# ScalarE's first guess of reciprocal roots at two seams of a fused two-layer kernel, moved transposes, and sums moved from GpSimd to VectorE

## The chip, the cores and the metric

The kernel runs on one core of a Trainium2 chip. The metric is the device time of one execution, in microseconds (us). The kernel before took 3251.36 us, the median of three executions (3250.76 to 3253.78).

The engines of the core are named as the profile names them: PE (TensorE, matrix products and transposes; PEld is its weight load), DVE (VectorE), ACT (ScalarE), POOL (GpSimd) and SP (SyncE, which here only issues DMAs).

## The reference

Two layers follow each other on x, 32 sequences of 128 tokens with 512 channels each, all float32.

```python
# layer 0
h   = ln(x) + silu(cond) @ W_ada.T            # one shift per sequence
q, k, v = h @ Wqkv.T                          # 16 heads of 64; q and k are normalised per head
x   = x + softmax(q k / 8) v @ Wout.T
tok = x.reshape(4096, 512)
gate = softmax(tok @ Wgate.T)                 # 8 experts
vals, idx = top_k(gate.T, 512)                # each expert takes its best 512 tokens
g   = ln(tok[idx])
y   = gelu_tanh(g @ fc1[e].T) @ fc2[e].T      # 512 -> 2048 -> 512, for each expert e
tok = tok.at[idx].add(y * vals)
# layer 1
n   = ln(x) * (1 + scale1) + shift1           # scale, shift = cond @ w_adaln1.T, per sequence
x   = x + attention(n) @ wo.T                 # 16 heads of 32
n   = ln(x) * (1 + scale2) + shift2
x   = x + gelu(n @ w1.T) @ w2.T               # 512 -> 2048 -> 512
```

Every `ln` needs the reciprocal square root of (variance + 1e-5) of each token; the change concerns how some of these are computed.

## The kernel before

**Stages.** Layer 0's attention goes by pairs of sequences. Then the router finds each expert's 512 tokens. Then come the experts 0 to 7 (function `expert(e, after)`), and then layer 1 in 16 groups of two sequences each (function `group(g)`). The stage of the experts begins at about 1086 us of the span, layer 1 at about 1916 us. At both seams the products of the next stage need the results of the last DMAs of the one before, so that PE has nothing else to do.

**Order of the work.** The kernel is written as a list of operations: each has its engine or engines (with an estimate of its time), what it reads and writes, and a priority. A planner (class `Sched`) goes through this list when the program is built, and gives each engine a fixed order of instructions. Where an operation may go to one of two engines (`also`), the planner chooses by its estimates. So an edit of one operation's priority or engine can move others too. The helper `tt` (L1106) makes an elementwise sum or difference of two tiles on DVE or on POOL; all of them appear in the profile with the line L1109 (DVE) or L1110 (POOL). All transposes have the line L1085.

**Normalisation.** `normed` (L311) takes a list of tiles of 128 tokens. For each it does the statistics (L317, L318, on DVE), then for all tiles of the list together variance + eps (L320) and `newton` (L293): a first guess of the reciprocal root by integer arithmetic on the bits of the float (L299), and three rounds of Newton's method of three operations each (L303, L305, L307). These are ten small operations on DVE in a chain, on one column per tile. The tile is then normalised (L1796 in the experts, xng; L2127 in layer 1, a_0n and so on), transposed by PE in four blocks of 128x128 (tpg; a_0t), and the four blocks are copied from PSUM with scale and shift by DVE and ACT in turn (L1806 and L1808, gT; L2137 and L2139, nT and n2T).

**An expert.** Four tiles xg of 128 tokens each are gathered by indirect DMAs that POOL issues (L1740). Expert 0's tiles are normalised in two pairs (names ng_0 and ng_1 in the profile), those of the later experts in one list of four. The two matrix products are done with seven block products in place of eight. So there are sums of blocks beside them: of gT (tg, the four sums at L1814 to L1817), of the fc1 weights (s, four POOL sums for each quarter m, L1763 to L1766), of the fc2 weights (t, L1785 to L1788: twelve sums t1, t2 and fc2_12 per expert, all on POOL), and of the products' results (h and hs). The first matrix goes in four quarters m = 0 to 3; a quarter is seven products u1, u2, u6, u7, u5, u4, u3 (L1838, PE, eight matmuls each), which DVE combines in the same order (v and h, L1843). ACT does the gelu (L1849), and the h and hs sums follow. The second matrix is the down products d (L1902), 32 matmuls each. Within expert 0 DVE also makes the token lists of the later experts (`expert_tokens`, L1666: oh L1684, pi on PE L1704, idx L1710), and the norms and transposes of expert 1.

**The seam into layer 1.** The scale and shift of all sequences come from products of the condition (pad), which are copied to pads, transposed by PE (ptd), and evicted with bias by four DVE operations (ss, L2029). `bias0` (L2109) is eight matmuls pb for the output bias, which DVE adds to bo_t (L2112). `norm_T` (L2122) is the normalisation, transposition and eviction of a group's two sequences; it stands before the attention (a1, dst nT) and before the MLP (a2, dst n2T, whose first product is m, L2363).

## Time and profile before

The profiled execution took 3251.28 us, of which 3249.5 us are the span that the profile shows.

| what | value |
|---|---|
| median of three executions | 3251.36 us |
| profiled execution, its span | 3251.28 us, 3249.5 us |
| mean clock granted to PE | 0.995 |
| PE busy | 98% of the span, 21786 matmuls |
| DVE, ACT, POOL busy | 69%, 29%, 22% |
| largest waits of PE | 11.9, 11.9, 5.3, 4.2, 1.4 us |
| span time of the first product of expert 0, of the first qk of layer 1 | 1101.02 us, 1923.56 us |

The busy row of the page gives for each engine its busy time and its share of the span. The table of waits names for an engine, its operation and line, what it waited for: the total, how often and the longest. The timeline gives the start of a piece of work from the span's start, its duration, and in brackets how long the engine had been idle before it and what ended that. A window gives the busy time of each engine in a stretch of the span, then the clock that PE was granted (1.00 is full speed), the share of DMA time and the GB/s moved. Numbers of buffers are left out of the names: ng_0 in the profile stands for the first norms of expert 0 and ng_1 for its second pair and for those of expert 1.

### The profile page before, as it was taken

Reading aid. Unit: us, or ns where it says so; the run is one execution under the profiler, and the core shown is the slowest. Engines: PE = TensorE matmul, PEld = TensorE weight load, DVE = VectorE, ACT = ScalarE, POOL = GpSimd, SP = SyncE. Lnnn points to the kernel's source line nnn. Section 1 sums busy time; section 2 is a strip of 40 time slices with the busy share of each in tenths; the row PEclk is TensorE's granted clock in tenths of the full one; section 3 lists DMA queues with packets and bytes.
Section 4 is the critical chain, followed back from the end, with each engine's and each line's share of the span. In section 5 each row is a group of like instructions: output and inputs, shape, how many; then the busy total and the mean of one; then the engine's idle time right before and its main releaser. Section 6 shows DMA issues by size and latency. Waiting matters only on the chain. (4 is left out here: it accounts for less than half of the span.)

```text
span 3249.5 us, 55816 instructions
## 1 busy us (share of the span) xinstructions
PE 3198.8 (98%) x21786; PEld 2556.4 (79%) x21786; DVE 2251.1 (69%) x4849; ACT 956.6 (29%) x2292; POOL 713.4 (22%) x563
## 2 busy tenths in 40 slices
PE   8999999999999899999999999999999999999999
PEld 4665666555557788888888878999999999999998
DVE  7877776978677888656666547666666666666665
ACT  3333333344431122221222213333333333333332
POOL 0111111000024457766676510000000000000000
PEclk9999999999999899999999999999999999999999
DMA  4122112221125523434333462333333333333343
GB/s 172 53 80 65 62 56 80 87 85 63 61 78 195 169 76 100 120 107 120 92 107 104 138 203 90 106 101 102 101 103 102 101 98 99 101 102 102 104 137 105
DMA packets 247122, 335.39 MB, mean 103 GB/s; under 512 B 22082, under 2 KB 156738, under 8 KB 246338
## 3 DMA queue, kind: packets, MB, share of 16 engines
q1 hardware_dynamic: 239394, 314.30, 29.7%
q0 software_dynamic: 7168, 16.91, 2.8%
q8 instruction: 174, 2.85, 0.4%
q14 instruction: 98, 0.80, 0.1%
q10 hardware_dynamic: 288, 0.52, 0.1%
HBM read 277.01 MB, written 54.66 MB: 102 GB/s over the span
## 5 line engine op out<-in xcount | busy, mean ns | idle before, releaser
L2318 POOL TENSOR_TENSOR hi_t<-hi_t,inv 128x512 f32<-128x512 f32 x32 | 40.7, 1273 | 1225.9 <-DVE inv L1120 1225.9
L2374 ACT ACTIVATE m<-m,prm 128x128 f32<-128x128 f32 x512 | 162.0, 390 | 235.8 <-DVE m L2368 235.7
L1902 PE MATMUL d<-fc,h 128*128 128x256 f32 x992 | 219.0, 380 | 0.6 <-DVE v L1843 0.6
L1902 PEld LDWEIGHTS d<-fc,h 128*128 128x128 f32 x992 | 187.9, 190 | 26.1 <-DVE v L1843 0.8
L1849 ACT ACTIVATE h<-h,prm 128x256 f32<-128x256 f32 x256 | 114.9, 500 | 259.8 <-DVE h L1843 259.7
L1838 PE MATMUL u<-gT,fc 128*128 128x256 f32 x768 | 178.6, 383 | 1.0 <-ACT gT L1808 1.0
L1838 PEld LDWEIGHTS u<-gT,fc 128*128 128x128 f32 x768 | 147.3, 192 | 21.8 <-ACT gT L1808 1.4
L2368 DVE TENSOR_TENSOR m<-mu,m 128x512 f32<-128x512 f32 x128 | 87.9, 687 | 106.8 <-PE m L2363 104.0
L1284 ACT ACTIVATE sq<-qk 128x512 f32<-128x512 f32 x128 | 80.7, 632 | 232.1 <-DVE qk L1322 227.9
L2368 DVE TENSOR_TENSOR mu<-mu,m 128x512 f32<-128x512 f32 x96 | 65.9, 686 | 88.2 <-PE m L2363 88.2
L2363 PE MATMUL m<-n2a,w_s 128*128 128x128 f32 x1024 | 124.9, 275 | 0.0
L2424 PE MATMUL n<-w_t,m 128*128 128x256 f32 x512 | 123.0, 379 | 0.0
L1838 PE MATMUL u<-tg,s 128*128 128x256 f32 x512 | 120.9, 379 | 0.9 <-DVE tg L1109 0.9
L2363 PE MATMUL m<-n2T,w 128*128 128x128 f32 x1024 | 119.8, 275 | 1.4 <-ACT n2T L2139 1.4
L1843 DVE TENSOR_TENSOR h<-v,u 128x512 f32<-128x512 f32 x128 | 86.3, 681 | 48.8 <-PE u L1838 47.3
L2363 PEld LDWEIGHTS m<-n2T,w 128*128 128x128 f32 x1024 | 118.2, 192 | 2.4 <-ACT n2T L2139 1.6
L2363 PEld LDWEIGHTS m<-n2a,w_s 128*128 128x128 f32 x1024 | 119.5, 192 | 0.0
L2424 PE MATMUL n<-w_t,ms 128*128 128x256 f32 x512 | 117.8, 382 | 0.0
L1318 PE MATMUL q<-wqkv,hT 128*128 128x512 f32 x240 | 114.6, 608 | 0.4 <-DVE oT L1470 0.4
L2424 PE MATMUL n<-w,m 128*128 128x256 f32 x512 | 114.7, 382 | 0.0
L1318 PE MATMUL q<-wqkv,hsb 128*128 128x512 f32 x240 | 113.9, 597 | 0.1
L1902 PE MATMUL d<-t,hs 128*128 128x256 f32 x512 | 113.4, 379 | 0.0
(1161 smaller groups left out, 7501.2 us busy)
## 6 DMA issues: line engine op xcount, KB each, us to landing
w_t<-t2d SPq DMA_DIRECT2D x256, 256.0 KB, 3.3
w<-in_w_dram SPq DMA_DIRECT2D x192, 256.0 KB, 4.8
fc<-in_fc_dram SPq DMA_DIRECT2D x64, 512.0 KB, 4.7
fc<-in_fc_dram SPq DMA_DIRECT2D x32, 1024.0 KB, 5.5
x<-in_x_dram SPq DMA_DIRECT2D x32, 256.0 KB, 3.4
xT<-in_xT_dram SPq DMA_DIRECT2D x32, 256.0 KB, 2.7
otd<-oT SPq DMA_DIRECT2D x32, 256.0 KB, 2.1
ol<-otd SPq DMA_DIRECT2D x32, 256.0 KB, 3.5
```

The costliest lines, as they stand in the source:

```text
L1284: sch.op(ACT, act_us(D), lambda: nc.scalar.activation(sq.t, qk[i][j].t, AF.Square), w=[sq], r=[qk[i][j]], prio=pr, job=job)
L1318: nc.tensor.matmul(ps[m].t, lhs()[:, k, :], rhs[0](k), start=(k == 0), stop=(k == 1))
L1838: nc.tensor.matmul(ps[n].t[:, t, :], lhs()[:, k, t * P : (t + 1) * P], rhs.t[:, k, :], start=(k == 0), stop=(k == 1))
L1843: sch.op(DVE, dve_us(D), lambda: nc.vector.tensor_tensor(o_.t, a_.t, ps[n].t, ALU.add), w=[o_], r=[a_, ps[n]], prio=pr, job=job)
L1849: sch.op(ACT, act_us(HQ, 1), lambda t=t, c=c: nc.scalar.activation(o_.t[:, t, :], o_.t[:, t, :], AF.Gelu_apprx_tanh, bias=col("b1s", e * 1 ...
L1902: nc.tensor.matmul(ps[n].t[:, j, :], lhs[m].t[:, k, t * P : (t + 1) * P], rhs.t[:, 2 * m + k, :], start=(m == 0 and k == 0), stop=(m == NM ...
L2318: sch.op(POOL, pool_us(D), lambda inv=inv: nc.gpsimd.tensor_tensor(hi_b.t, hi_b.t, flat(inv), ALU.add), w=[hi_b], r=[inv], prio=pr + 197, ...
L2363: nc.tensor.matmul(ps[n].t[:, u, :], l1w[what].t[:, k, (NQ * q + u) * P : (NQ * q + u + 1) * P], rhs()[:, k, :], start=(k == 0), stop=(k = ...
L2368: sch.op(DVE, dve_us(D), lambda: nc.vector.tensor_tensor(o_.t, a_.t, ps[n].t, ALU.add), w=[o_, *more], r=[a_, ps[n]], prio=pq_, job=job)
L2374: sch.op(ACT, act_us(S, 1), lambda u=u, c=c: nc.scalar.activation(o_.t[:, u, :], o_.t[:, u, :], AF.Gelu, bias=col("b1", c), scale=1.0), w= ...
L2424: nc.tensor.matmul(ps[n].t, Ah[lhs][c // NQ].t[:, c % NQ, :], b_.t[:, k, :], start=(c == 0), stop=(c == 7))
```

## The change

1. A new function `guessed` computes the first guess with two operations of ACT, Ln of the variance and Exp of -0.5 times that (both scaled by a power of two), and one round of Newton on DVE. It takes the place of the integer guess and three rounds, in expert 0's norms, and in both norms of group 0 of layer 1. There the tiles are also handled one by one and no longer in pairs, but for expert 0's tiles 2 and 3. The variances are gathered in `seen` and added to a flag tile (hi_b) that is read at the kernel's end.
2. In expert 0, the transposes of tiles 2 and 3 get an earlier place on PE (directly behind u1 and u2 of m = 0), the gsel copies a later one (behind the tg sums), and the tg sums stay on DVE.
3. The twelve t sums of expert 0 go from POOL to DVE, at a priority of the first products. The planner in turn gives seven h and hs sums of m = 0 and 1 to POOL.
4. The statistics of expert 1's tiles wait for expert 0's last tg sum, and its transposes get a later priority: they come behind the first down products of expert 0.
5. At the seam into layer 1, `bias0` is split in two halves with the transposes ptd between them, the ss evictions come behind the norms of group 0, and the bo_t addition comes later. An empty ACT operation makes the table of Exp be loaded behind the copies to pads.

```diff
@@ -310,3 +310,22 @@
-    def normed(self, srcs, name, pr, job, cols=D):
+    def guessed(self, mv, v, n, name, pr, job):
+        nc, sch = self.nc, self.sch
+        z, y, t = self.sml(name + "z", n), self.sml(name + "y", n), self.sml(name + "t", n)
+        us = dve_us(n)
+        var = lambda: mv.t.rearrange("p (n two) -> p n two", two=2)[:, :, 1]
+        sch.op(ACT, 0.3, lambda: nc.scalar.activation(z.t, var(), AF.Ln, bias=self.lnc[:, 0:1], scale=2.0**-32),
+               w=[z], r=[mv], prio=pr, job=job, table="exp")
+        sch.op(ACT, 0.3, lambda: nc.scalar.activation(y.t, z.t, AF.Exp, bias=self.lnc[:, 1:2], scale=-0.5),
+               w=[y], r=[z], prio=pr, job=job, table="exp")
+        sch.op(DVE, us, lambda: nc.vector.scalar_tensor_tensor(t.t, y.t, -0.5, y.t, ALU.mult, ALU.mult),
+               w=[t], r=[y], prio=pr, job=job)
+        sch.op(DVE, us, lambda: nc.vector.tensor_tensor(t.t, t.t, v.t, ALU.mult),
+               w=[t], r=[t, v], prio=pr, job=job)
+        sch.op(DVE, us, lambda: nc.vector.scalar_tensor_tensor(y.t, t.t, 1.5, y.t, ALU.add, ALU.mult),
+               w=[y], r=[t, y], prio=pr, job=job)
+        return y
+    def normed(self, srcs, name, pr, job, cols=D, act=False, after=()):
@@ -316,3 +335,3 @@
             st = self.sml(f"{name}st{i}", 6)
-            sch.op(DVE, dve_us(D), lambda st=st, s=s: nc.vector.bn_stats(st.t, s.t[:, :cols]), w=[st], r=[s], prio=pr, job=job)
+            sch.op(DVE, dve_us(D), lambda st=st, s=s: nc.vector.bn_stats(st.t, s.t[:, :cols]), w=[st], r=[s, *after], prio=pr, job=job)
             sch.op(DVE, 0.17, lambda st=st, i=i: nc.vector.bn_aggr(mv.t[:, 2 * i : 2 * i + 2], st.t),
@@ -322,2 +341,5 @@
             w=[v], r=[mv], prio=pr, job=job)
+        if act:
+            self.v = v
+            return mv, self.guessed(mv, v, n, name, pr, job)
         return mv, self.newton(v, n, name, pr, job)
@@ -1035,2 +1057,8 @@
     nc.vector.memset(ones_f, 1.0)
+    st.lnc = const_tile("lnc", (P, 2))
+    nc.vector.memset(st.lnc[:, 0:1], EPS * 2.0**-32)
+    nc.vector.memset(st.lnc[:, 1:2], -16 * math.log(2.0))
+    seen = const_tile("seen", (P, 8))
+    nc.vector.memset(seen, 0.0)
+    seen_b = stands(seen)
     iota_j = const_tile("iota_j", (P, P), I32)
@@ -1724,2 +1752,10 @@
+    seen_v = []
+    def saw(pr, job, after):
+        for v, at, n in seen_v:
+            sch.op(DVE, 0.15, lambda v=v, at=at, n=n: nc.vector.tensor_scalar(seen[:, at : at + n], v.t, 2.0**-32, None, ALU.mult),
+                   w=[(seen_b, at)], r=[v, *after], prio=pr, job=job)
+        seen_v.clear()
     def expert(e, after):
@@ -1768,3 +1804,3 @@
         if e:
-            mv, y = st.normed(xg, f"ng_{e}", pe_, job, cols=D)
+            mv, y = st.normed(xg, f"ng_{e}", pe_, job, cols=D, after=sums0 if e == 1 else ())
             stat = [(mv, y, h) for h in range(NH)]
@@ -1772,5 +1808,8 @@
             stat = []
-            for z in range(2):
-                mv, y = st.normed(xg[2 * z : 2 * z + 2], f"ng_{e}_{z}", pe_ + z, job, cols=D)
-                stat += [(mv, y, h) for h in range(2)]
+            def norm0(hs, pr, after=()):
+                mv, y = st.normed([xg[h] for h in hs], f"ng_{e}_{hs[0]}", pr, job, cols=D, act=True, after=after)
+                stat.extend((mv, y, i) for i in range(len(hs)))
+                seen_v.append((st.v, hs[0], len(hs)))
+            norm0((0,), pe_ - 3)
+            norm0((1,), pe_ - 3)
         if 0 < e < E - 1:
@@ -1788,7 +1827,12 @@
                 tt(lambda o_=o_, hs=hs: o_.t[:, hs, :], lambda a_=a_, hs=hs: a_.t[:, hs, :], lambda b_=b_, hs=hs: b_.t[:, hs, :],
-                   ALU.subtract, D, [(o_, h)], [(a_, h), (b_, h)] + ([] if e else [y]), pe_ - 600 + 1000 + n, job, POOL, False)
+                   ALU.subtract, D, [(o_, h)], [(a_, h), (b_, h)], pe_ - 600 + 1000 + n if e else PR + 25, job,
+                   POOL if e else DVE, False)
+        px = (pe_ - 3, pe_ - 3, pe_ - 1, pe_ - 1) if e == 0 else (pe_ + 53 if e == 1 else pe_,) * NH
         Bg = {(j, l): row(f"gT_{e}_{j}{l}", (P, 2, HQ)) for j in (1, 2) for l in (1, 2)}
         for h in range(NH):
+            if e == 0 and h == 2:
+                norm0((2, 3), pe_ - 1, [xn])
             xn, tp = row(f"xng_{e}_{h}"), bank(f"tpg_{e}_{h}")
@@ -1797,4 +1841,4 @@
                 xn.t, xg[h].t[:, :D], mv.t[:, 2 * z : 2 * z + 1], y.t[:, z : z + 1], ALU.subtract, ALU.mult),
-                w=[xn], r=[xg[h], mv, y], prio=pe_ - 1 if e == 0 and h < 2 else pe_, job=job)
-            sch.op(PE, 4 * TR, lambda tp=tp, xn=xn: transpose4(tp.t, xn.t), w=[tp], r=[xn], prio=pe_, job=job)
+                w=[xn], r=[xg[h], mv, y], prio=px[h], job=job)
+            sch.op(PE, 4 * TR, lambda tp=tp, xn=xn: transpose4(tp.t, xn.t), w=[tp], r=[xn], prio=px[h], job=job)
             for c in range(DC):
@@ -1809,5 +1853,3 @@
                 sch.op(DVE, dve_us(P, 2), lambda ev=ev: ev(DVE), also=[(ACT, act_us(P, 2), lambda ev=ev: ev(ACT))],
-                       w=[(q, (c % 2, h % 2))], r=[tp], prio=pe_, job=job)
-            sch.op(DVE, 0.16, lambda h=h: nc.vector.tensor_copy(gs.t[:, h : h + 1], xg[h].t[:, D + e : D + e + 1]),
-                   w=[(gs, h)], r=[xg[h]], prio=pe_ + 2, job=job)
+                       w=[(q, (c % 2, h % 2))], r=[tp], prio=px[h] + (0.5 if e == 0 else 0), job=job)
         Tg = {n: row(f"tg_{e}_{n}", (P, 2, HQ)) for n in (1, 2, 4)}
@@ -1815,6 +1857,11 @@
                            (Tg[4], Bg[2, 1], Tg[2])):
-            tt(lambda o_=o_: o_.t, lambda a_=a_: a_.t, lambda b_=b_: b_.t, ALU.subtract, D, [o_], [a_, b_], pe_ + 3, job)
+            tt(lambda o_=o_: o_.t, lambda a_=a_: a_.t, lambda b_=b_: b_.t, ALU.subtract, D, [o_], [a_, b_], px[3] + 3, job,
+               also=e > 0)
         Tg[3] = Bg[1, 2]
+        for h in range(NH):
+            sch.op(DVE, 0.16, lambda h=h: nc.vector.tensor_copy(gs.t[:, h : h + 1], xg[h].t[:, D + e : D + e + 1]),
+                   w=[(gs, h)], r=[xg[h]] + ([Tg[4]] if e < 2 else []), prio=pe_ + 2, job=job)
         if e == 0:
             sums0.append(Tg[4])
+            saw(PR + 5, job, [Tg[4]])
             expert_tokens(1, RP + 750, job)
@@ -2025,2 +2072,4 @@
     sch.op(PE, 4 * TR, lambda: transpose4(flat(ptd), pads.t), w=[ptd], r=[pads], prio=LB - 822, job=LJ)
+    sch.op(ACT, 0.01, lambda: None, r=[pads], prio=LB - 822, job=LJ, table="exp")
     for n, (ss, ssb, nm) in enumerate(((ss1, ss1_b, "b_adaln1"), (ss2, ss2_b, "b_adaln2"))):
@@ -2030,3 +2079,3 @@
                 ss[:, 4 * h : 4 * h + 4, :], ptd.t[:, :, (2 * n + h) * 32 : (2 * n + h) * 32 + NB], 1.0 - h,
-                bcast(prm[:, at : at + 4], NB), ALU.add, ALU.add), w=[(ssb, h)], r=[ptd], prio=LB - 822, job=LJ)
+                bcast(prm[:, at : at + 4], NB), ALU.add, ALU.add), w=[(ssb, h)], r=[ptd], prio=LB - 818.5, job=LJ)
@@ -2105,4 +2154,4 @@
-    def bias0():
-        for i in (1, 2):
+    for i in (1, 2):
+        def bias0(i=i):
             for c in range(DC):
@@ -2110,5 +2159,5 @@
                                  start=(c == 0), stop=(c == DC - 1))
-    sch.op(PE, mm_us(D, DC), bias0, w=[pb0], r=[bvb] + [l1w[f"o{i}{j}"][1] for i in (1, 2) for j in (1, 2)], prio=LB - 821, job=LJ)
+        sch.op(PE, mm_us(QD, DC), bias0, w=[(pb0, i)], r=[bvb] + [l1w[f"o{i}{j}"][1] for j in (1, 2)], prio=LB - 821, job=LJ)
     sch.op(DVE, dve_us(D), lambda: nc.vector.tensor_tensor(bo_b.t, bo_b.t, pb0.t, ALU.add), w=[bo_b], r=[bo_b, pb0],
-           prio=LB - 815, job=LJ)
+           prio=LB - 700, job=LJ)
@@ -2121,5 +2170,5 @@
-    def norm_T(srcs, dst, ss, ssb, b0, name, pr, job, off=0):
+    def norm_T(srcs, dst, ss, ssb, b0, name, pr, job, off=0, act=False):
-        mv, y = st.normed(srcs, name, pr, job)
+        mv, y = st.normed(srcs, name, pr, job, act=act)
         for i, s in enumerate(srcs):
@@ -2178,3 +2227,8 @@
         nT = [row(f"nT_{g}_{j}", (P, 2, GT)) for j in range(2)]
-        norm_T(x2, nT, ss1, ss1_b, b0, f"a1_{g}", pr - 820, job)
+        if g:
+            norm_T(x2, nT, ss1, ss1_b, b0, f"a1_{g}", pr - 820, job)
+        else:
+            for i in range(GB):
+                norm_T([x2[i]], nT, ss1, ss1_b, b0, f"a1_{g}_{i}", pr - 820 + i, job, i, True)
+                seen_v.append((st.v, 4 + i, 1))
@@ -2338,3 +2392,11 @@
         n2T = [row(f"n2T_{g}_{j}", (P, 2, GT)) for j in range(2)]
-        norm_T(x3, n2T, ss2, ss2_b, b0, f"a2_{g}", po_ + 5, job)
+        if g:
+            norm_T(x3, n2T, ss2, ss2_b, b0, f"a2_{g}", po_ + 5, job)
+        else:
+            for i in range(GB):
+                norm_T([x3[i]], n2T, ss2, ss2_b, b0, f"a2_{g}_{i}", po_ + 5 + i, job, i, True)
+                seen_v.append((st.v, 6 + i, 1))
+            saw(pr + 196, job, n2T)
+            sch.op(DVE, 0.16, lambda: nc.vector.tensor_tensor(hi_b.t[:, :8], hi_b.t[:, :8], seen, ALU.add),
+                   w=[hi_b], r=[hi_b, seen_b], prio=pr + 198, job=job)
         for i in range(GB):
```

## The prediction

> **What bounds the kernel now.** I read the page's engine row first, then the waits of PE over the whole span, then the windows and the timeline around each long wait.
>
> ```profile
> PE 3198.8 (98%) x21786; PEld 2556.4 (79%) x21786; DVE 2251.1 (69%) x4849; ACT 956.6 (29%) x2292; POOL 713.4 (22%) x563
> ```
>
> PE works for 3198.8 of 3249.5 us, so only some 51 us of the span are idle on it, and no product is added or removed by the change. What can be gained is idle time of PE, and time in which PE runs at half clock because it was idle. The waits of PE (us in total, times, longest) say where it lies:
>
> ```profile
> PE tpx L1085 <- DVE xn L1383: 11.9, 2, 10.6
> PE tpg L1085 <- DVE xng L1796: 11.9, 1, 11.9
> PE a_0t L1085 <- DVE a_0n L2127: 5.3, 1, 5.3
> PE u L1838 <- DVE v L1843: 4.2, 1, 4.2
> PE m L2363 <- ACT n2T L2139: 1.4, 1, 1.4
> ```
>
> The first is the kernel's start, which the change leaves. The other four are its places: the seam into expert 0, the seam into layer 1, the middle of expert 0, and the first MLP of layer 1. The seam into expert 0 in the timeline (start, duration, work, [idle before]):
>
> ```profile
> 1092.60 0.69 DVE L317 BATCH_NORM_STATS2 ng_0st<-xg 128x6 f32<-128x512 f32 x1 [5.51 <-DMA xg<-tok,idx]
> 1094.04 0.69 DVE L317 BATCH_NORM_STATS2 ng_0st<-xg 128x6 f32<-128x512 f32 x1 [0.49 <-DMA xg<-tok,idx]
> 1095.24 0.17 DVE L299 TENSOR_SCALAR ng_0y<-ng_0v 128x2 int32<-128x2 int32 x1
> 1097.20 1.26 DVE L1796 TENSOR_SCALAR xng<-xg,ng_0mv,ng_0y 128x512 f32<-128x512 f32 x2
> 1098.10 1.94 PE L1085 MATMUL tpg<-ident,xng 128*128 128x128 f32 x8 [11.91 <-DVE xng L1796]
> 1101.02 6.83 PE L1838 MATMUL u<-gT,fc 128*128 128x256 f32 x20 [0.98 <-ACT gT L1808]
> ```
>
> Of the 11.91 us, the gather (DMA) ends what comes before 1092.60; only 1092.60 to 1098.10 is arithmetic, and in it the ten small operations from 1095.24 to 1097.20 take 1.96 us, 0.196 each. They begin only when tile 1, whose gather landed 1.44 us after tile 0's, has its statistics. The middle of expert 0:
>
> ```profile
> 1128.20 4.93 POOL L1110 TENSOR_TENSOR t<-fc,fc 128x512 f32<-128x512 f32 x4
> 1128.60 14.86 DVE L1109 TENSOR_TENSOR hs<-h,h 128x512 f32<-128x512 f32 x1
> 1137.99 4.92 POOL L1110 TENSOR_TENSOR fc<-fc,fc 128x512 f32<-128x512 f32 x4
> 1144.87 3.75 PE L1838 MATMUL u<-tg,fc 128*128 128x256 f32 x8 [4.15 <-DVE v L1843]
> 1148.41 2.67 PE L1838 MATMUL u<-gT,s 128*128 128x256 f32 x8
> 1148.95 1.64 DVE L1109 TENSOR_TENSOR hs<-hs,h 128x512 f32<-128x512 f32 x1
> ```
>
> One DVE sum, 0.68 us elsewhere, takes 14.86 us: as long as the twelve t sums on POOL (1128.20 to 1142.9, 1.23 each) run without a gap. Behind it no product is combined, PSUM fills, and PE stops at 1140.7 for 4.15 us. The windows (us; busy PE, PEld, DVE, ACT, POOL; PE clock; DMA share; GB/s) show the after-effect:
>
> ```profile
> 1130.00:1140.00 10.00, 10.00 (x48) 8.81 (x47) 10.00 (x1) 0.00 (x0) 10.00 (x9) 1.00 0.34 114
> 1140.00:1144.80 4.80, 0.71 (x4) 0.28 (x2) 4.80 (x5) 0.65 (x2) 4.14 (x4) 0.83 0.00 0
> 1144.80:1148.40 3.60, 3.53 (x8) 2.83 (x9) 3.60 (x7) 2.42 (x6) 0.00 (x0) 0.50 0.29 76
> ```
>
> The clock is 0.50 for 3.6 us after the stall: eight matmuls take 3.75 there, and 1.89 warm. The seam into layer 1:
>
> ```profile
> 1918.65 0.88 DVE L2029 SCALAR_TENSOR_TENSOR ss<-ptd,prm 128x128 f32<-128x128 f32 x4
> 1921.20 1.00 DVE L2127 TENSOR_SCALAR a_0n<-x,a_0mv,a_0y 128x512 f32<-128x512 f32 x2
> 1921.80 1.97 PE L1085 MATMUL a_0t<-ident,a_0n 128*128 128x128 f32 x8 [5.30 <-DVE a_0n L2127]
> 1923.56 1.70 PE L2197 MATMUL qk<-nT,wq 128*128 128x128 f32 x8
> ```
>
> Statistics of both sequences begin at 1916.45; the four ss evictions stand amid the ten small operations, from 1918.65 to 1919.44.
>
> **What the Trainium skill says.** "TensorE: Matmul & The Clock Gate", part 1: an idle window of about 3.4 us halves the clock, and about 3.4 us of work restore it. The trace agrees: 0.50 for 3.6 us after a stall of 4.15 us. "GPSIMD Engine Reference", section 8: GpSimd shares its SBUF interfaces with VectorE and contends with VectorE instructions that have two SBUF inputs. The trace agrees (14.86 us), while h<-v,u with one input in PSUM stays at 0.67 beside POOL. "ScalarE: Activation LUTs", table sets: Ln and Exp lie in one set, so the pair needs one table. No run here shows the pair alone; the order of the changed kernel's instructions has no more table loads. Price, from its section on what ACT_TABLE_LOAD costs: 280 ns + 0.833 ns an element with a pointer bias, so by estimate 0.28 for 128x1. Rows of the trace bound it below: Ln of 128x512 takes 597 ns and Exp 630, less 512 x 0.833 = 427, so 0.17 to 0.20.
>
> **The change part by part.**
>
> Guess by ScalarE, expert 0. Of ten small operations three stay (3 x 0.196 = 0.6); Ln and Exp come in, 2 x 0.28 = 0.56, bounded 0.37 to 0.56, and two hand-overs between engines. For tile 0 the guess lies beside tile 1's wait and statistics (1094.04 to 1094.95). So: tile 0's aggregate is done at 1093.5; tile 1's statistics end about 1095.0; three small operations 0.6 and xng 0.63 give 1096.3; with the hand-over tpg_0 starts about 1096.5, not 1098.10. Tile 1's three operations and xng follow (1.2, 1097.5), its transposes at half clock end about 1098.5 (before 1100.04), and the first product comes at about 1099.8, not 1101.02: -1.2. Tiles 2 and 3 now are transposed after u1_0_0 and u2_0_0, ahead of the half product u1_0_1 that stood there. Their first eviction comes about 1105.9, not 1108.39 (-2.5). From there a chain on DVE (evictions, tg sums, oh, pi) of some 13.5 us leads to the next PE wait at 1122, with PE's products filling it; one half product (0.87) more has to be filled in later. Net -2.5 + 0.9 = -1.6; from -0.3 (only the clock phase) to -2.5. The gsel copies behind the tg sums (4 x 0.13) and the four seen operations (4 x 0.16) cost nothing so long as DVE has slack before 1124; otherwise 1.2 of DVE, which I count in the next sum.
>
> t sums to VectorE, expert 0. POOL loses 12 x 1.23 = 14.8; DVE gets 12 x 0.68 = 8.2. The planner in turn gives seven h and hs sums of expert 0 to POOL: DVE -7 x 0.68 = -4.8, POOL +7 x 1.25 = 8.8. What goes: the wait of 4.15, the half clock (3.75 - 1.89 + 2.67 - 1.89 = 2.6), and two waits for DVE ahead of the transposes and the first down product (0.71 + 0.60): 8.0 together. What is late next? Window 1124 to 1164: DVE was busy 39.6 of 40; 39.6 - 14.2 (held) + 8.2 - 4.8 = 28.8, with 1.2 from above 30. PE needs 40 - 4.15 - 2.6 = 33.2 there. POOL now runs about 17 sums in it (seven moved, two more hs, eight s sums of expert 1). Beside four s sums (1148.70 to 1155.1) three DVE sums took 1.64, 1.16 and 1.75: 2.5 us more, 0.63 for each POOL sum. About half of DVE's work is of two SBUF inputs, so I take 17 x 0.63 / 2 = 5.4: 35.4 against 33.2, DVE 2.2 behind. PE can run on: in the trace the hold began at 1128.6 and PE stopped at 1140.7, so banks cover some 10 us. What shows is a wait at the turn to the down products, where the last sums are due; I charge 1.0 (0 to 4). DVE's new sums wait for the fc2 loads at its head, with all combinations queued behind; these loads had landed by about 1117 and the sums are reached near 1124, so nothing, and 1 for each us that a load were later than 1124 plus the cover. One sum, hs2 of m=0, waits for POOL behind three gathers (1.27 each): about 2 us, inside the cover. Sum -7.0, from -4 to -8.
>
> Transposes of expert 1 behind the first down products: same PE work; the products lie between, so the transposes' inputs have more time. Zero, unless expert 1's gT then is late; the rest of the down products (7 us for each 32 matmuls) covers that.
>
> Layer 1 seam. Out of DVE's chain go the ss evictions (0.79) and seven small operations (1.4), in comes the ACT hop; the first tile no longer waits for the second's statistics (0.9). Transposes start about 1919.5, not 1921.80. But ss is now behind both normalisations, and the eviction of a_0t needs it: about 1921, so the first qk comes at about 1921.9, not 1923.56: -1.7 (-0.8 to -2.6; the lower end if the bo_t sum or a table load stood ahead of Ln). The ptd transposes move ahead of half of pb, 0.6 before 1.2 us of work, with nothing on SP reordered.
>
> First MLP. Per tile and with seven operations fewer, n2T is ready at least 1.4 earlier for tile 0: the wait of 1.37 goes, and I take -1.2 (0 to -1.4), since the two ACT operations queue with exps.
>
> Sum: -1.6 - 7.0 - 1.7 - 1.2 = -11.5. The profiled execution took 3251.28 us (span 3249.5 and 1.8 around it), 0.1 below the median 3251.36. So 3251.3 - 11.5 = 3239.8 us.
>
> **The rivals.** *Half of the middle comes back*: DVE sums are held by POOL sums at 0.63 each always, not half the time: 10.7, so 40.7 against 33.2, 7.5 behind; the cover takes it up to the turn, where about 4.5 shows. 3244.3. For it: the DVE was full in this window. Against: seven DVE sums are gone. *The seams do not pay*: ScalarE's hops cost as much as the seven operations; only the middle stays: 3251.3 - 7.0 = 3244.3. For it: each hop is two hand-overs, none of which the trace shows for so small an operation; against: the first tile's guess has tile 1's statistics beside it. *VectorE becomes the bound* (slower): each of the 17 POOL sums holds a DVE sum to its end, at the price of the t sums (14.2 / 12 = 1.18): 20.1, so 50.1 against 33.2, 16.9 late; with the half clock of 2.6 again 19.5 lost, where 8.0 was: +11.5, less 4.5 from the seams, 3258.3. It decides from 12.5 of loss, that is about 0.75 us per POOL sum. Against it: the POOL sums of the hs kind wait for each other and for ACT, so gaps are left. *The change doesn't do what it says*: Ln and Exp drag table loads of 1.28 us into each seam; the order of instructions shows none added.
>
> **How the numbers follow.** Measurements of this kernel tell about 0.2%, 6.5 us, from no change: faster is below 3244.9, slower above 3257.8. Forecast 0.65 (own range 3236 to 3244); half of the middle 0.15 (3243 to 3247); seams not paying 0.10 (3242 to 3246); VectorE the bound 0.06 (3251 to 3259); anything else 0.04. The range 3236 to 3247 holds the first three. Faster: 0.65 + half to two thirds of the next two = 0.83; same 0.12; slower 0.05.
>
> **What would show it.** No DVE sum of over 3 us in expert 0 and no PE wait for v there; clock 1.00 through its products; the first tpg 1.5 us and the first qk 1.7 us nearer to the DMA that feeds them; no wait of m for n2T. It would be wrong if PE waits for DVE at u or at the first d for over 4 us, or if a new wait for ACT stands at a seam.

## The result and the profile after

The changed kernel takes 3241.82 us (median of 9, 3239.60 to 3245.76), where the kernel before took 3251.97 us in the executions beside it (median of 9). The ratio is 0.9967, with a 95% interval of 0.9959 to 0.9976: 8 to 13 us won. The prediction was 3239.8 us, so 11.5 won. Its profiled execution took 3242.52 us, 8.8 less than the one before; the table of stages below is of these two.

The engine row of the page after:

```profile
PE 3199.2 (99%) x21786; PEld 2559.9 (79%) x21786; DVE 2242.1 (69%) x4854; ACT 959.7 (30%) x2302; POOL 705.3 (22%) x557
```

PE does the same work in a span of 3240.5 us: 41 us idle where 51 were. The waits of PE over the whole span, after:

```profile
PE tpg L1113 <- ACT ng_1y L320: 9.8, 1, 9.8
PE u L1885 <- DVE tg L1137: 2.2, 2, 1.7
PE pi L1732 <- DVE oh L1712: 1.0, 2, 0.8
```

The wait for v (4.2) and the one for n2T (1.4) are gone, and those at the two seams are shorter by 2.1 and 2.5. The first line names ACT, whose Exp for tile 1 ends at 1096.17; what tpg needs is tile 0's xng, which ends at 1096.16. Two waits are longer: u for the tg sums (2.2 where 0.9 was) and pi for oh (1.0 where 0.8 was).

Where the time went is read best by setting the same matmul of both traces side by side: all 21786 are recorded in each, so the n-th matmul of a name in one is the n-th in the other. (The last product of the stage before the experts differs by up to 2.9 us from profile to profile, whatever was edited behind that point. So each stage is measured from its own start. Each row ends where the matmul that it names begins.)

| stage, from start to start | before, us | change, measured | change, predicted |
|---|---|---|---|
| first statistics of expert 0 to first product u | 8.43 | -1.93 | -1.2 |
| to the last matmul of u7 in the second quarter (m = 1) | 25.50 | +3.95 | -0.4 |
| to the last matmul of the sixth of expert 0's seven down products d | 81.51 | -8.97 | -7.0 |
| to the end of expert 7 | 698.69 | 0.00 | 0 |
| to the seventh product qk of layer 1's group 0 (of n1b) | 23.39 | -1.21 | -1.7 |
| to the 32nd matmul n of group 1 | 162.49 | -0.99 | -1.2 |

The sum is -9.2. The middle of expert 0, the third row, gave more than predicted, and the first seam took the difference. Later text calls the last row group 0, in whose MLP the wait for n2T was. The windows that held the stall before, in the changed kernel (us; busy PE, PEld, DVE, ACT, POOL; PE clock; DMA share; GB/s):

```profile
1124.00:1140.00 16.00, 16.00 (x72) 13.90 (x71) 15.31 (x23) 6.54 (x15) 10.60 (x9) 0.94 0.62 199
1140.00:1160.00 20.00, 20.00 (x94) 17.66 (x93) 19.69 (x34) 5.00 (x11) 15.38 (x12) 1.00 0.18 55
```

PE has no gap, and from 1140 on full clock; VectorE is still full (19.69 of 20), but nothing is waited for. The 0.94 in the first window comes from half clock between 1122.5 and 1125.9, which was not there before. The timeline of the first seam, after, shows where that and the +3.95 come from:

```profile
1094.06 0.29 ACT L320 ACTIVATE ng_0y<-ng_0z,lnc 128x1 f32<-128x1 f32 x1
1096.31 2.20 PE L1113 MATMUL tpg<-ident,xng 128*128 128x128 f32 x8 [9.82 <-ACT ng_1y L320]
1099.29 6.73 PE L1885 MATMUL u<-gT,fc 128*128 128x256 f32 x16 [0.78 <-ACT gT L1852]
1109.53 1.55 DVE L1137 TENSOR_TENSOR tg<-gT,gT 128x512 f32<-128x512 f32 x1
1115.52 1.72 POOL L1138 TENSOR_TENSOR s<-fc,s 128x512 f32<-128x512 f32 x1
1116.28 5.45 DVE L1712 TENSOR_TENSOR oh<-iota_jb,lo 128x1024 bf16<-128x1024 bf16 x4
1121.78 0.36 PE L1732 MATMUL pi<-val,oh 128*128 128x8 bf16 x8 [0.78 <-DVE oh L1712]
1122.00 1.60 PE L1885 MATMUL u<-gT,s 128*128 128x256 f32 x4
```

The first transposes come at 1096.31, as predicted (1096.5). But the tg sums then run beside GpSimd's s sums from the first to the last: 6.7 us for the four, where they took 5.6 before. The s sums end at 1117.24 here and at 1116.98 before, so much of the earlier start of the tg sums is used up against them: the first oh, beside the last s sum, takes 2.04, and the three behind it 1.21 each. The four together take 5.45 (before 4.62), and the last pi matmuls start at 1121.78, 0.34 ahead of before (0.53 counted from the first statistics). There are 0.87 us of products more behind them here, and these run at half clock: the first four matmuls take 1.60, where before the four at this place took 1.11.

### The profile page after: what moved, and what is told of

Same layout as the page of the kernel before. It is cut to its first block, busy times and chain, and to the rows that moved or that the text cites. A ratio compares the mean times of both kernels' runs of the same rounds, so it can differ in the third digit from the quotient of the medians.

```text
span 3240.5 us, 55814 instructions
## 1 busy us (share of the span) xinstructions
PE 3199.2 (99%) x21786; PEld 2559.9 (79%) x21786; DVE 2242.1 (69%) x4854; ACT 959.7 (30%) x2302; POOL 705.3 (22%) x557
```

## The experiments

Each time is compared with the kernel before run beside it (3251.7 to 3252.4). Stages are the rows of the table above, as differences to the profile of before. "Seam" is the sum of its first two rows, and "middle" is its third.

**Run 1, the t sums alone.** The kernel before with

```diff
-   ALU.subtract, D, [(o_, h)], [(a_, h), (b_, h)] + ([] if e else [y]), pe_ - 600 + 1000 + n, job, POOL, False)
+   ALU.subtract, D, [(o_, h)], [(a_, h), (b_, h)] + ([] if e else [y]), pe_ - 600 + 1000 + n if e else PR + 25, job,
+   POOL if e else DVE, False)
```

> The kernel before with one edit: the twelve t sums of expert 0 go to VectorE. Theory (the middle of expert 0 paid because no run of twelve GpSimd sums is left that can hold a VectorE sum): no VectorE sum over 2.5 us in expert 0, no wait of 4.2 us of PE for v, about 7 us of the 8.8 won; 3245 against 3252. The rest, some 2 us, would be the transposes of expert 1, which stay ahead of the down products here. Rival (the other parts made the room for the sums: the later statistics of expert 1 and the moved transposes): VectorE gets 3.4 us more than it gives away, PE waits at the turn to the down products for 3 us or more, and only 3 to 5 us are won, 3247 to 3249.

3250.41, ratio 0.9995 (0.9987 to 1.0004): no difference that can be told. The wait for v is gone, and 6.9 us are won up to the last first product; then 4.8 are given back ahead of the down products. The timeline of this run:

```profile
1158.95 1.19 DVE L305 TENSOR_TENSOR ng_1t<-ng_1t,ng_1v 128x4 f32<-128x4 f32 x1
1161.06 2.99 PE L1085 MATMUL tpg<-ident,xng 128*128 128x128 f32 x12 [4.84 <-DVE xng L1797]
```

The small operations of expert 1's norms, 0.16 each when GpSimd is idle, take 1.2 beside its sums. Expert 1's transposes stand ahead of the down products here, wait 4.84 us for what these operations lead to, and half clock follows. Both expectations were too high (7 and 3 to 5 us), but the rival was right that the t sums alone leave a wait of over 3 us at this turn.

**Run 5, the later transposes alone.** The kernel before with

```diff
-   mv, y = st.normed(xg, f"ng_{e}", pe_, job, cols=D)
+   mv, y = st.normed(xg, f"ng_{e}", pe_, job, cols=D, after=sums0 if e == 1 else ())
...
+   px = pe_ + 53 if e == 1 else pe_
```

and `px` in place of `pe_` as the priority of expert 1's normalisations, transposes and evictions, `px + 3` of its tg sums.

> The kernel before with one part: the statistics of expert 1 wait for expert 0's last tg sum, and its transposes come behind the first down products. The t sums stay on GpSimd. Theory (the run of twelve GpSimd sums is the cause of the stall; the moved transposes only keep a full VectorE from being waited for at the turn to the down products): a VectorE sum of over 10 us is still there, PE still waits about 4 us for v, and only the two waits ahead of the transposes and the first down product go, 1 to 2 us: 3250 to 3251 against 3252. Rival (the moved transposes are themselves the larger part): 4 us or more, 3248 or less.

3250.06, ratio 0.9991 (0.9982 to 0.9999); middle -2.7. The stall is where it was (PE waits 4.3 for v), under this sum:

```profile
1126.08 15.52 DVE L1109 TENSOR_TENSOR hs<-h,h 128x512 f32<-128x512 f32 x1
```

**Run 6, both together.** Both edits above on the kernel before.

> The kernel before with two parts together: the t sums on VectorE, and expert 1's statistics and transposes later. Both seams stay as they were. Theory (from the run with the t sums alone, which won 7.0 us up to the last first product and gave back 4.8 at the transposes, and from the changed kernel, which gave back nothing): the two together win 8.5 to 9 us, 3243 against 3252, nearly all that the whole change wins. Rival (each part adds on its own): what the t sums alone won, 1.8, and the transposes' own 1 to 2, so 3248 to 3249.

3244.91, ratio 0.9978 (0.9969 to 0.9988), middle -8.6. Alone the parts are worth 2.1 and 2.7 in this stage, together 8.6: each removes what the other runs into. The theory holds for the stage; the whole kernel gains 7.5 of the 10 us of the whole change, a little less than the 8.5 expected. (Whole times, with 1.8 and 2.4 us for the parts alone, have intervals too wide to show by themselves that the two together are worth more than their sum. The stages show it, one profile for each run. What the later statistics and the later transposes are worth each was not separated.)

**Run 9, no VectorE sums beside GpSimd's run.** The kernel before with the h and hs sums of m = 0, 1 of expert 0 on GpSimd alone, the t sums as they were:

```diff
-   tt(lambda o_=o_: o_.t, lambda a_=a_: a_.t, lambda b_=b_: b_.t, op_, D, [o_], [a_, b_], pr + 15 + n, job)
+   tt(lambda o_=o_: o_.t, lambda a_=a_: a_.t, lambda b_=b_: b_.t, op_, D, [o_], [a_, b_], pr + 15 + n, job,
+      *((POOL, False) if e == 0 and m < 2 else ()))
```

> The kernel before with one edit: the t sums stay on GpSimd, in the same run of twelve, and the h and hs sums of expert 0's first two quarters may only go to GpSimd (they stand behind the t sums there). Theory (the stall came because a VectorE sum with two SBUF inputs met GpSimd's run; combinations with one input in PSUM do not mind it): GpSimd still works without a gap for some 15 us, but no VectorE sum is held through it, and PE does not wait 4 us for v in this stretch: 6 to 7 us won up to the last first product, as with the t sums on VectorE, whatever is given back later at the turn to the down products. Rival (GpSimd's load itself, or VectorE's amount of work, made the stall): PE waits for v or for h as before, 2 us won or less there.

3255.38, ratio 1.0010 (1.0003 to 1.0016), slower, and the theory as I had put it falls. No VectorE sum is held, but the timeline of this run shows what is:

```profile
1128.37 4.96 POOL L1110 TENSOR_TENSOR t<-fc,fc 128x512 f32<-128x512 f32 x4
1132.08 12.30 DVE L320 TENSOR_SCALAR ng_1v<-ng_1mv 128x4 f32<-128x4 f32 x1
1153.23 1.19 DVE L307 SCALAR_TENSOR_TENSOR ng_1y<-ng_1t,ng_1y 128x4 f32<-128x4 f32 x1
1156.65 3.75 PE L1838 MATMUL u<-tg,s 128*128 128x256 f32 x8 [7.71 <-DVE h L1843]
```

An operation on four columns, with a single SBUF tensor as input, is held 12.30 us; it takes 0.17 otherwise. Ahead of it, statistics (0.66) and h<-v,u (0.67) pass beside the same run without loss. So a VectorE sum with two SBUF inputs isn't needed for the hold, and neither is a large amount of work. The rival's forecast, that PE waits as before, came true; of its two causes, GpSimd's load is the one that this trace supports.

The 12.30 is not all of the stall: it costs PE only 0.90 us (up to 1145.22). The 7.71 come behind the rest of the same chain: of nine small operations up to 1154.42, seven take 1.1 to 1.2 us each, beside nine more GpSimd sums, and h<-v,u stands behind them on VectorE. These nine sums follow each other with only two pauses, of 0.08 us, and still hold an operation for about one sum only.

**Run 2, without the first seam's edits.** The changed kernel with `normed` in pairs and `newton`, the transposes, gsel copies and tg sums of expert 0 as before, of which the diff shows a part:

```diff
-   norm0((0,), pe_ - 3)
-   norm0((1,), pe_ - 3)
+   for z in range(2):
+       mv, y = st.normed(xg[2 * z : 2 * z + 2], f"ng_{e}_{z}", pe_ + z, job, cols=D)
+       stat += [(mv, y, h) for h in range(2)]
...
-   if e == 0 and h == 2:
-       norm0((2, 3), pe_ - 1, [xn])
```

> The changed kernel with the norms, transposes, gsel copies and tg sums of expert 0 as they were before; all other parts stay. Theory (in the trace of the changed kernel the seam into expert 0 is 1.9 us later, not earlier, when the second quarter's products begin: 2.0 won at the first product, of which 0.6 is left at the last token product, then half a product more and a stretch of 3.4 us at half clock): 1.9 us faster than the changed kernel, 3239.9. Rival (the prediction: the seam gains 1.6, the half clock is chance): 1.6 slower, 3243.4.

3240.94, ratio 0.9966 (0.9954 to 0.9978), the same as the changed kernel within both intervals. The first row of the table is back at -0.1, and the seam is +1.0 where it is +2.0 in the changed kernel. Neither the theory (1.9 faster) nor the prediction's gain of 1.6 shows: these edits are worth nothing that can be measured.

**Run 11, the changed kernel once more.**

> The changed kernel once more, beside the others on one chip, for its time there and for what changes from one profile of it to the next. Theory (the stretch of half clock at 1122 follows from PE's waits there and not from chance): it is there again, the second quarter's products begin 1 to 2 us later after the statistics than before, the stages from there to the end of the down products win 8.5 to 9.0, group 0 wins 1.0; the time is 10 us, 0.3%, below the kernel before. Rival (the half clock is chance): none at 1122, and the seam into expert 0 wins 0.5 to 1.

3242.15, ratio 0.9968 (0.9956 to 0.9981). Seam -0.1, middle -8.2, group 0 -1.0, and no half clock at 1122. The theory, that PE's waits decide the half clock, falls: PE waits longer for oh here (2.0 in three waits, 1.0 in two in the first profile). The 0.5 to 1 us of the rival don't show either. So the half clock there is not fixed: of three profiles with this seam (the changed kernel twice, and run 7) two have it. The seam is +2.0, +1.0 and -0.1 in these, and between 0 and +1.4 in the five whose first seam is the old one and in its old order (before, runs 1, 5, 6 and 9). The means, 1.0 and 0.6, say nothing won.

**Run 3, the token list later.** Changed kernel with

```diff
-   expert_tokens(e + 1, pe_ + 1 if e > 1 else RP + 660, job, sums0)
+   expert_tokens(e + 1, pe_ + 1, job, sums0)
```

> The changed kernel, with the token list of expert 2 (four oh operations on VectorE, 5.4 us, and 32 small products of PE) planned behind expert 0's first products, and not between the tg sums and the first combinations. Theory (the seam's gain is lost because PE waits for this list at 1120 to 1122 and then falls to half clock): waits of 1.0 and the 1.7 of the half clock go, and the gain at the first product comes through; 2.5 to 3.5 us faster than the changed kernel, 3238.3 to 3239.3. Rival (VectorE is full until the down products begin, so the 5.4 us come back as a wait there): the same or up to 3 us slower, 3242 to 3245.

3244.37, ratio 0.9977 (0.9970 to 0.9983), some 2.5 slower than the changed kernel, at the edge of what can be told. The seam is -2.8: with the list out of the way the gain comes through. But PE then waits for the same oh ahead of the down products (the waits and half clock leave the middle at -0.2). In this run's timeline:

```profile
1149.13 5.67 DVE L1712 TENSOR_TENSOR oh<-iota_jb,lo 128x1024 bf16<-128x1024 bf16 x3
1158.76 0.38 PE L1732 MATMUL pi<-val,oh 128*128 128x8 bf16 x8 [3.55 <-DVE oh L1712]
```

The theory was right on the seam, the rival on the sum.

**Run 8, the list later still.** The changed kernel with

```diff
-   expert_tokens(e + 1, pe_ + 1 if e > 1 else RP + 660, job, sums0)
+   expert_tokens(e + 1, pe_ + 1 if e > 1 else pe_ + 58, job, sums0)
```

> The changed kernel with expert 2's token list later still: its PE part stands behind expert 0's down products, its oh operations on VectorE stand at the end of the first products, where nothing waits for them. Theory (the seam's gain of 1.7 came through when the list was out of the way, and it was lost only because PE waited 4.6 us for oh ahead of the down products and fell to half clock): no wait of PE for oh, no half clock at 1122, 2.5 to 4 us faster than the changed kernel, 3238 to 3239.3. Rival (VectorE is full up to the down products, so the transposes of expert 1 or the first combinations there come late): a new wait of PE for xng or v of 3 us or more, 3241 or more.

3243.35, ratio 0.9969 (0.9957 to 0.9982), not faster than the changed kernel. Seam -2.4 and middle -9.0 came, and 7.5 are lost in expert 1, where expert 2's norms now meet expert 1's twelve t sums. In this run's timeline:

```profile
1214.63 5.55 POOL L1138 TENSOR_TENSOR t<-fc,fc 128x512 f32<-128x512 f32 x4
1218.50 2.94 DVE L339 TENSOR_SCALAR ng_2v<-ng_2mv 128x4 f32<-128x4 f32 x1
1224.09 4.94 POOL L1138 TENSOR_TENSOR t<-fc,t 128x512 f32<-128x512 f32 x4
1230.30 1.19 DVE L307 SCALAR_TENSOR_TENSOR ng_2y<-ng_2t,ng_2y 128x4 f32<-128x4 f32 x1
1235.03 3.78 PE L1885 MATMUL u<-tg,s 128*128 128x256 f32 x8 [3.76 <-DVE h L1890]
```

It is the stall of run 9 again, one expert on: a chain of small operations of which eight take 1.1 to 1.2 us, and one 2.94, ahead of the combination that PE needs. The last eight t sums, from 1224.09 to 1234.10, follow each other without a pause, as the twelve of the kernel before did; yet they hold each operation for one sum and not for the whole run.

**Run 10, expert 1's t sums on VectorE too.** As run 8, with

```diff
-   pe_ - 600 + 1000 + n if e else PR + 25, job,
-   POOL if e else DVE, False)
+   pe_ - 600 + 1000 + n if e > 1 else PR + 25, job,
+   POOL if e > 1 else DVE, False)
```

> The changed kernel with expert 2's token list behind expert 0's first products and expert 1's twelve t sums on VectorE too. Theory (the later list was worth 2.5 us at the seam, and was lost in expert 1, where GpSimd's next run of twelve t sums held the small operations of expert 2's norms 1.2 to 2.9 us each until PE waited 3.8 for h and fell to half clock; without that run nothing is held): no wait of PE for h in expert 1, no half clock there, 3 to 5 us faster than the changed kernel run beside it, about 3237. Rival (VectorE has too much to do in expert 1 as well): a wait for v or h of 2 us or more in expert 1, within 2 us of the changed kernel.

3245.62, ratio 0.9980 (0.9971 to 0.9989), slower than the changed kernel. Expert 1's products run without a wait for h, but then 10.5 us are lost in one place: expert 2's transposes, still ahead of expert 1's down products, wait for VectorE, and half clock lasts 10.2 us. The longest of this run's waits of PE there:

```profile
PE tpg L1113 <- DVE v L1890: 3.4, 1, 3.4
```

The place is that of run 1, one expert on, but the cause is another. The transposes' inputs xng were there by 1247.1; what ended the wait is a combination v at 1257.2, which stands on VectorE behind the four oh of a token list (1249.2 to 1257.3, one of them 2.28 us beside a GpSimd sum). That is VectorE with too much to do at this turn, as the rival had it.

**Run 12, the edits in every expert.** The changed kernel with

```diff
-   expert_tokens(e + 1, pe_ + 1 if e > 1 else RP + 660, job, sums0)
+   expert_tokens(e + 1, pe_ + 58, job, sums0)
...
-   pe_ - 600 + 1000 + n if e else PR + 25, job,
-   POOL if e else DVE, False)
+   PR + 25, job, DVE, False)
...
-   px = (pe_ - 3, pe_ - 3, pe_ - 1, pe_ - 1) if e == 0 else (pe_ + 53 if e == 1 else pe_,) * NH
+   px = (pe_ - 3, pe_ - 3, pe_ - 1, pe_ - 1) if e == 0 else (pe_ + 53,) * NH
```

> The changed kernel with three of its edits made in every expert and not in the first alone: all t sums on VectorE, all transposes of the next expert behind the first down products, and all token lists of the next expert but one behind the first products. Theory (what the two runs before lost came each time from the next expert: the run of twelve GpSimd sums in expert 1, and transposes of expert 2 that waited for VectorE ahead of the down products; with neither left, nothing is given back): the seam's 2.5 us and the middle's 9 come through and stay, no PE wait of over 1 us and no half clock between 1110 and 1890; 3 to 5 us faster than the changed kernel, 3237 to 3239. Rival (VectorE, with 8.2 us more in each expert, is now waited for in each): a wait of PE for VectorE that comes again with each expert, several us slower than the changed kernel.

3247.48, ratio 0.9988 (0.9981 to 0.9994). Seam -2.8, middle -9.0; then 13.1 are lost over experts 1 to 7. The theory's premise came true: no VectorE operation of this run takes longer than 2.31 us, where in the changed kernel, with the t sums of experts 1 to 7 on GpSimd, single ones take 3.2 to 8.2 us in every expert from 1 on (at no cost to PE: the fourth row of the table is 0.00). But neither theory nor rival named the cause of the loss. PE waits 8.3 us between 1110 and 1900, all but 0.8 of it for GpSimd:

```profile
PE u L1884 <- POOL s L1138: 7.5, 5, 2.0
```

The 3.4 us of half clock there cost about 1.7 more. What makes up the remaining 3, and why GpSimd is late with twelve sums less in each expert, stays open.

**Run 4, Newton in place of ScalarE.** The changed kernel, tiles one by one, with

```diff
         if act:
             self.v = v
-            return mv, self.guessed(mv, v, n, name, pr, job)
```

> The changed kernel with the integer guess and three rounds of Newton in place of ScalarE's guess, at all its places; tiles still one by one. Theory (ScalarE's guess pays only at the seam into layer 1, because at the seam into expert 0 the tg sums cannot end before GpSimd's s sums do): up to 1.5 slower, 3242 to 3243.3, or no slower if the half clock at 1122 does not come. Rival (each place pays seven small operations less a hop of two hand-overs, about 1.0 us, at three places): 3 us slower, 3244.8.

3249.33, ratio 0.9992 (0.9983 to 1.0000): 7.5 slower than the changed kernel, far more than both expected. This isn't the old norm, since a chain of its own for tile 0 and for tile 1 doubles their small operations. Seam +5.7, the next +2.8, group 0 +0.8; the profiled execution is 4.0 above the median of this run, so these three say too much. The timeline of this run:

```profile
1109.05 1.19 DVE L303 SCALAR_TENSOR_TENSOR ng_2t<-ng_2y 128x2 f32<-128x2 f32 x1
1114.34 0.66 PE L1112 MATMUL tpg<-ident,xng 128*128 128x128 f32 x4 [3.77 <-DVE xng L1839]
```

GpSimd's first s sum starts at 1106.40, and from then on five of the six small operations left take 1.1 to 1.2 us in place of 0.16. In the changed kernel this chain is over by 1102.4, before GpSimd starts (1105.47). The tg sums here come after the last s sum (1116.82) and take 0.67 to 0.69 each, which shows from the other side what the s sums cost them in the changed kernel.

**Run 7, without the second seam and group 0.** The changed kernel with

```diff
-   if g:
-       norm_T(x2, nT, ss1, ss1_b, b0, f"a1_{g}", pr - 820, job)
-   else:
-       for i in range(GB):
-           norm_T([x2[i]], nT, ss1, ss1_b, b0, f"a1_{g}_{i}", pr - 820 + i, job, i, True)
-           seen_v.append((st.v, 4 + i, 1))
+   norm_T(x2, nT, ss1, ss1_b, b0, f"a1_{g}", pr - 820, job)
```

the same for a2, `bias0` in one piece, ss evictions and bo_t at their old priorities.

> The changed kernel with the seam into layer 1 and group 0's norms as they were before. Theory (in the traces the seam won 1.2 and group 0 1.0): 2.2 us slower than the changed kernel, 3244.0 where that is 3241.8. Rival (the prediction: 1.7 and 1.2): 2.9 slower, 3244.7. If the two waits only move to a later place, no slower.

3244.54, ratio 0.9976 (0.9965 to 0.9987): 2.7 above the changed kernel, between what the two expected, though the two intervals overlap. Group 0's 1.0 is gone exactly. At the seam the old order gives 0 to +2.3 in six profiles (mean 0.9), and the new one -0.7 to -2.0 in seven (mean -1.3): 2.2 apart.

## Why the prediction was right, and where it was not

**The size.** Forecast -11.5, measured -10.2. Most of it is the middle of expert 0, as predicted. The terms are off in both directions: 2.0 too little in the middle and 1.6 too much at the first seam nearly cancel. That the sum came so near is in part luck.

**ScalarE's guess.** Ln and Exp take 0.29 us each, as the Trainium skill's price gives in "ScalarE: Activation LUTs", what ACT_TABLE_LOAD costs (0.28); the lower bound from wide rows (0.17) was too low. No table load came in (35 in both kernels). The hop is short: a VectorE operation begins 0.04 us after Exp ends (1101.78, 1101.82). The first product was 1.9 earlier and not 1.2. Of these 0.7 us, 0.5 lie in the evictions: the forecast left 1.3 between the last transpose of tile 1 and the first product, and it took 0.78 (0.98 before).

**The net of the first seam: this step failed.** The prediction said "Net -2.5 + 0.9 = -1.6", on the ground that a chain of 13.5 us from the first eviction would start earlier and keep its length. Counted from the first statistics, its start moved by -2.1 and its end, at the last pi, by -0.5: it stretched from 13.7 to 15.3 us, since the tg sums (1.1 more) and the first oh (0.8 more) are slowed until GpSimd's s sums end, and those didn't move. Of the 0.5 nothing that can be measured is left behind it (runs 2 and 11); the seam gains 2.4 to 3.7 in runs 3, 8, 10 and 12, where the end of that chain, oh and pi, stands later.

**The t sums.** The 8.0 of waits and half clock went, and more (8.2 to 9.0 in the profiles of all kernels with both parts, but run 3, which waits for the list, and run 4). The 1.0 charged for a wait at the turn was not needed. The holding itself was larger than assumed. By the excess of VectorE's sums over 0.68 and of expert 1's small operations over 0.16 between 1124 and 1163, it is 11.7 us in the changed kernel (16.7 before), beside the 17 GpSimd sums that were counted on, where 5.4 was forecast and the rival "half of the middle comes back" had 10.7. So that rival's premise was true, and its stall still did not come.

**The transposes at "zero": mis-sized.** They are the reason why it did not come. What GpSimd held at the end were small operations of expert 1's norms (4.8 of the 11.7), and with the transposes behind the down products PE did not come to them until 1185.9. Run 1 without them loses 4.8 there. They are worth 6.5 of the 8.6 once the t sums have moved, and 2.7 alone. The words "the products lie between, so the transposes' inputs have more time" had the mechanism; the sum gave it no value. Two errors met here, a holding put at half its size and a remedy put at nothing.

**The form that is held.** The prediction let GpSimd hold only operations with two SBUF inputs, and took the sums alone. Its own profile has more: the two xng of tiles 2 and 3, with one SBUF tensor as input, take 2.92 us beside the first s sums (1105.44), and the first two took 1.26 ahead of them.

**Slips in the working.** "0.50 for 3.6 us" is the length of the window that was asked for; the half clock behind the stall lasted 6.8 us, from 1143.2 to 1150.0. The price of 2.6 us for it holds, since it was taken from the products. The rival "half of the middle comes back" charges the 1.0 us at the turn twice: its own terms give 3243.3.

**Layer 1.** Forecast -1.7 and -1.2; measured -1.2 against one profile of before (-2.2 between the means) and -1.0. The timeline of the changed kernel:

```profile
1912.58 0.66 PE L1113 MATMUL a_0t<-ident,a_0n 128*128 128x128 f32 x4 [2.76 <-DVE a_1v L339]
1913.54 0.68 DVE L2078 SCALAR_TENSOR_TENSOR ss<-ptd,prm 128x128 f32<-128x128 f32 x3
1914.62 1.67 PE L2251 MATMUL qk<-nT,wq 128*128 128x128 f32 x6 [0.29 <-ACT nT L2188]
```

As forecast, ss is what the eviction now waits for: qk begins 2.1 earlier counted from the first statistics, where 1.7 was forecast. One us of that is lost again in the first two products qk, and by the clock, not by a wait: half clock from 1914.4 to 1917.8 covers 14 of their matmuls (0.21 us apart, 0.11 at full clock), where before, from 1921.4 to 1924.8, it covered the transposes and six. The forecast had no term for this.

**The slower rival** (VectorE the bound) did not come: VectorE is at 19.69 of 20 and PE has no gap. A late VectorE did cost time in runs 1, 8, 9 and 10, where PE waited 3.4 to 7.7 us for it.

## What to carry to other kernels

Price a small operation of VectorE by what GpSimd does at that moment: here 0.16 us alone, 1.2 beside a row of its sums, and in the worst case the rest of the row (12.30 in run 9). A gain at the head of a seam counts only if the next wait moves too, so follow it to the point at which the slowest chain is due. Two edits that each show almost nothing alone can be worth the whole gain together, if each takes away what the other would run into.

## What the hardware showed that was not expected

A 128x4 operation of VectorE with one SBUF tensor as input waited 12.30 us beside a run of independent GpSimd sums (run 9), while statistics of a 128x512 tile and combinations with PSUM ran there at full speed. "GPSIMD Engine Reference", section 8, of the Trainium skill names two SBUF inputs and a two-port mode as what contends, and gives no length; the second may be the form here, which no run tells. Nor do the runs tell when the hold lasts: three profiles show it through a run of twelve (14.86, 15.52 and 12.30 us), but in run 8 eight sums without a pause held small operations for about one sum each (1.19). The half-clock stretches of PE were 3.4, 6.8, 10.2, 13.7, 17.1 and 20.5 us long in these traces, multiples of 3.41, but for the one at each trace's end. Two came without any idle time near 3.4 us: at 1122.5 in the changed kernel and at 1119.4 in run 7, after waits of 0.3 and 0.8 us between matmuls of 8 columns. The second profile of the changed kernel had waits of this kind, 2.0 us in all, and no such stretch.
